# Pairwise bilinear interaction on one core: a ring of five x tiles, paired loads of x, four stores a tile, products in place

## The chip, the cores and the metric

The kernel runs on one core of a Trainium2 chip. The metric is the device time of one execution in microseconds (us). A core has a matrix engine (PE, or TensorE), which multiplies and transposes into PSUM, and VectorE (DVE), ScalarE (ACT) and GpSimd (POOL), which work element by element; GpSimd works on SBUF alone here. SyncE (SP) only issues transfers. 16 DMA engines move data between HBM and SBUF. Transfers issued by SP, by ScalarE and by GpSimd wait in three queues, and each DMA engine serves all three.

## The reference

```python
def _L0_rec_ref(inputs, W):                  # inputs (4096, 32, 64), W (496, 64, 64), float32
    F = inputs.shape[1]
    idx_i, idx_j = np.triu_indices(F, k=1)
    vi = inputs[:, idx_i, :]
    vj = inputs[:, idx_j, :]
    vidots = jnp.einsum('bpd,pde->bpe', vi, W)
    return vidots * vj
```

Every sample has 32 fields of 64 numbers. For each of the 496 pairs of fields (i, j), i < j, field i is multiplied by that pair's own 64 x 64 matrix, and the result, element by element, by field j. The output has 4096 x 496 x 64 numbers, 520 MB; the inputs have 42 MB.

## The kernel before

**Tiles.** 128 samples are a tile, one to a partition; there are 32 tiles, and two of them (NB = 2) are a block of 256 neighbouring samples, which is loaded by one transfer of 2 MB. `xpool` holds two blocks. The partition p of a block holds samples 2p and 2p + 1, so a partition's 16 KB lie together in HBM.

**Steps.** The work of a tile is a list of 46 steps (L169): step (g, i, c0, m) covers up to 16 pairs of one field i (CH = 16), the pairs p0[i] + c0 to p0[i] + c0 + m. A step has two matmuls (L259), one for each half of the 64 outputs, from the transposed x (`xT`) and the transposed weights (`wT`) into one PSUM tile `ps` of two banks (four such buffers, shared with the transposes). In the trace one such float32 matmul counts twice. Then the step multiplies by field j. For most steps DVE does this straight out of PSUM into the output tile `ot` (L279). For seven steps of a tile, those of `aside` with c0 = 0, ScalarE copies the PSUM tile to SBUF (L276) and GpSimd multiplies (L277). For the first three tiles the copy goes into `ot` itself and the product is made in place; for all others it goes into a spare tile `tmp` of `tpool`, which has four buffers.

**Output.** The 496 pairs are cut into five groups of 90 to 105 (`bounds`, L45). Each group of a tile has an `ot` of `opool`, which has three buffers, and one store by SP (L284). The very first group goes out in two stores.

**Transposed x.** `turn_x` (L153) transposes eight fields at a time on PE (L159), and ScalarE copies the result three times into an `xT` (L163 to L165) of four buffers. This is traced six steps (AHEAD) before the first step that needs it.

**Weights.** `load_w` loads W in four chunks of 128 rows, of which `cuts` says which are used: 0 to 128, 128 to 256, 256 to 368, 368 to 496. `order_w` (L139) reorders a quarter of a chunk on DVE, GpSimd or ScalarE, `turn_w` transposes it (L148) and copies it into `wT` (L151). `wT` has two tiles, rows 0 to 384 and the last 128, so that a step across row 368 takes two pairs of matmuls. The raw chunks lie in buffers of `opool`, in `wT` and in the last tile. A table of places in the schedule (L198) says when the quarters of chunks 1 to 3 are reordered and turned.

**The order of the work.** The schedule (L185) interleaves the first three tiles (LEAD) group by group, and then takes the tiles one by one. The framework orders each engine's instructions by this program and by what is ready, and puts in the waits for buffers; `keep_in_program_order` pins an instruction behind all that its engine was given before.

**Loads of x.** Blocks 0 and 1 are loaded by SP at the start, with W. Each later block is one load, traced at step 6 (LATE) of the first tile of the block before it (block 2 at step 6 of tile 3). Blocks 2, 3, 4, 6, 8, 10 and 12 are loaded by ScalarE's queue (L81), not pinned: in the trace they are issued when the last product that reads the buffer ends. Blocks 5, 7, 9, 11, 13, 14 and 15 (`fifteen`, L71) are loaded by GpSimd's queue, pinned, in four transfers (`load_fifteen`, L100): 120 partitions, a transfer of a few bytes (`turn_engines`, L97), and the last 8 partitions in two parts of 16 fields. The 120 partitions are spread over 15 DMA engines, so one engine is spared. In those blocks a gap of 64 bytes parts a partition's two samples.

Of the kernel before, what the change touches and what calls it, by code (L numbers as in the profile page):

```python
# [8 lines left out]
F32 = mybir.dt.float32  # L9
# [3 lines left out]
def kernel(  # L13
# [15 lines left out]

    nc = tc.nc  # L30

    B, F, D = x.shape
    P = 128
    NB = 2
    assert 2 * D == P and B % (NB * P) == 0
    NBLK = B // (NB * P)
    NP = F * (F - 1) // 2
    E2 = D // 2
    BANK = 512
    CH = BANK // E2  # L40
    RUN = 8
    p0 = [i * (F - 1) - i * (i - 1) // 2 for i in range(F)]


    bounds = [0, p0[3], p0[6] + CH, p0[11], p0[17], NP]  # L45
    groups = list(zip(bounds[:-1], bounds[1:]))
    cap = max(b - a for a, b in groups)

    aside = (1, 3, 5, 7, 9, 11, 13)

    cuts = [0, P, 2 * P, NP - P, NP]
    wrows = list(zip(cuts[:-1], cuts[1:]))

    const = ctx.enter_context(tc.tile_pool(name="const", bufs=1))
    xpool = ctx.enter_context(tc.tile_pool(name="xpool", bufs=2))
    xtpool = ctx.enter_context(tc.tile_pool(name="xtpool", bufs=4))
    tpool = ctx.enter_context(tc.tile_pool(name="tpool", bufs=4))
    opool = ctx.enter_context(tc.tile_pool(name="opool", bufs=3))
    psum = ctx.enter_context(tc.tile_pool(name="psum", bufs=4, space=bass.MemoryType.PSUM))

    ident = const.tile([P, P], F32, tag="ident", name="ident")
    make_identity(nc, ident)

    xs = {}
# [4 lines left out]


    fifteen = (5, 7, 9, 11, 13, 14, 15)  # L71

    def new_x(blk: int):
        gap = 16 if blk in fifteen else 0
        wide = xpool.tile([P, NB * (F * D + 16)], F32, tag="xs", name=f"xs_{blk}")
        wide = wide[:, : NB * (F * D + gap)].rearrange("p (k n) -> p k n", k=NB)
        xs[blk] = wide[:, :, : F * D].rearrange("p k (f d) -> p k f d", d=D)

    def load_x(blk: int, eng, k0: int = 0, k1: int = NB):
        src = rows_of(x, blk).rearrange("(p k) f d -> p k f d", k=NB)  # L80
        eng.dma_start(out=xs[blk][:, k0:k1], in_=src[:, k0:k1])  # L81
# [4 lines left out]
    SWR = 120  # L86
# [13 lines left out]
    def load_fifteen(blk: int):  # L100
        rows = rows_of(x, blk).rearrange("(p k) f d -> p k f d", k=NB)
        dst = xs[blk]

        def part(ps: slice, fs: slice):
            tc.keep_in_program_order(nc.gpsimd.dma_start(out=dst[ps, :, fs, :], in_=rows[ps, :, fs, :]))  # L105

        part(slice(0, SWR), slice(0, F))
        turn_engines(1)
        for h in range(2):
            part(slice(SWR, P), slice(h * F // 2, (h + 1) * F // 2))  # L110


    wflat = w.rearrange("p d e -> p (d e)")
    raw, wT = {}, {}
    EU = 2 * BANK // P
    NU = E2 // EU


    def home_of(c: int, r: int):
        home, tag, n = (wrows[3][0], "w3", P) if c == 3 else (0, "w", 3 * P)  # L120
        if home not in wT:
            wT[home] = const.tile([P, n, E2], F32, tag=tag, name=f"wT_{home}")
        return wT[home][:, wrows[c][0] - home : wrows[c][0] - home + r, :]

    def load_w(c: int):

        a = wrows[c][0]
        if c == 2:
            raw[c] = home_of(c, P).rearrange("p r e -> p (r e)")
        else:  # L130
            pool, tag = (const, "w3") if c == 3 else (opool, "ot")
            raw[c] = pool.tile([P, D * D], F32, tag=tag, name=f"raw_{c}")
        nc.sync.dma_start(out=raw[c], in_=wflat[a : a + P])

    def order_w(c: int, k: int, copy):
        r = wrows[c][1] - wrows[c][0]
        rp = tpool.tile([P, EU, 2, D], F32, tag="tmp", name=f"rp_{c}_{k}")
        src = raw[c][:r, :].rearrange("p (d h e) -> p e h d", h=2, d=D)
        ins = copy(rp[:r], src[:, k * EU : (k + 1) * EU])  # L139
        if c > 0:  # L140
            tc.keep_in_program_order(ins)
        return rp

    def turn_w(c: int, k: int, rp, copy):
        r = wrows[c][1] - wrows[c][0]
        pt = psum.tile([P, EU, P], F32, tag="ps", name=f"ptw_{c}_{k}")
        for n in range(EU):
            nc.tensor.transpose(  # L148
                pt[:, n, :r], rp[:r, n].rearrange("p h d -> p (h d)"), ident[:r, :r]
            )  # L150
        copy(home_of(c, r)[:, :, k * EU : (k + 1) * EU], pt[:, :, :r].rearrange("p e r -> p r e"))  # L151

    def turn_x(blk: int, k: int, q: int, copy):  # L153


        pt = psum.tile([P, RUN // 2, P], F32, tag="ps", name=f"ptx_{blk}_{k}_{q}")
        for u in range(RUN // 2):
            f = q * RUN + 2 * u
            nc.tensor.transpose(  # L159
                pt[:, u, :], xs[blk][:, k, f : f + 2, :].rearrange("p f d -> p (f d)"), ident  # L160
            )
        xT = xtpool.tile([P, 2, RUN // 2, P], F32, tag="xT", name=f"xT_{blk}_{k}_{q}")
        copy(xT[:, 0], pt)  # L163
        copy(xT[D:, 1], pt[:D])  # L164
        copy(xT[:D, 1], pt[D:])  # L165
        return xT


    steps = [  # L169
        (g, i, c0, min(CH, F - 1 - i - c0))  # L170
        for i in range(F - 1)
        for c0 in range(0, F - 1 - i, CH)
        for g, (a, b) in enumerate(groups)
        if a <= p0[i] + c0 < b
    ]
    NS = len(steps)
    first = {}
    for s, (_, i, _, _) in enumerate(steps):
        first.setdefault(i, s)

    LEAD = 3
    NT = NBLK * NB
    sched = [  # L185
        (t, s) for g in range(len(groups)) for t in range(LEAD) for s in range(NS) if steps[s][0] == g
    ]
    sched += [(t, s) for t in range(LEAD, NT) for s in range(NS)]
    place = {ts: n for n, ts in enumerate(sched)}


    AHEAD = 6
    due: dict = {}
    for t in range(NT):
        for q in range(F // RUN):
            at = place[t, first[q * RUN]] - AHEAD
            due.setdefault(max(0, at), []).append(("x", t // NB, t % NB, q))
    for c, orders, turns in (  # L198
        (1, (2, 4, 8, 10), (4, 7, 12, 15)),
        (2, (16, 18, 25, 27), (30, 33, 36, 39)),  # L200
        (3, (46, 48, 50, 52), (56, 59, 62, 65)),
    ):
        for k in range(NU):
            due.setdefault(orders[k], []).append(("order", c, k))
            due.setdefault(turns[k], []).append(("turn", c, k))
    LATE = 6
    loads = {place[blk * NB, LATE]: blk + 1 for blk in range(2, NBLK - 1)}
    loads[place[LEAD, LATE]] = 2

    new_x(0)  # L210
# [4 lines left out]
    new_x(1)  # L215
# [5 lines left out]
    v, p, a = nc.vector.tensor_copy, nc.gpsimd.tensor_copy, nc.scalar.copy  # L221
    xT, rps = {}, {}
    xT[0, 0, 0] = turn_x(0, 0, 0, a)
    due[0] = [d for d in due[0] if d != ("x", 0, 0, 0)]
# [5 lines left out]
    ots = {}  # L230
    for s, (t, st) in enumerate(sched):
        blk, kt = divmod(t, NB)
        g, i, c0, m = steps[st]
        if s in loads:
            new_x(loads[s])
            if loads[s] in fifteen:
                load_fifteen(loads[s])
            else:
                load_x(loads[s], nc.scalar)
        for what, *args in due.get(s, ()):  # L240
# [4 lines left out]
            else:  # L245
                c, k = args
                rps[c, k] = order_w(c, k, ((v, v, p, v), (v, v, p, a))[k % 2][c])

        base, end = groups[g]
        pa = p0[i] + c0  # L250
        if pa == base:
            ots[t] = opool.tile([P, cap, D], F32, tag="ot", name=f"ot_{t}_{g}")
        ot = ots[t]
        ps = psum.tile([P, 2, CH, E2], F32, tag="ps", name=f"ps_{s}")
        for lo, hi in ((0, wrows[3][0]), wrows[3]):
            home, lo, hi = lo, max(pa, lo), min(pa + m, hi)
            if lo < hi:
                for h in range(2):
                    nc.tensor.matmul(  # L259
                        ps[:, h, lo - pa : hi - pa, :],  # L260
                        xT[blk, kt, i // RUN][h * D : (h + 1) * D, (i + h) % 2, i % RUN // 2, :],
                        wT[home][h * D : (h + 1) * D, lo - home : hi - home, :],
                        start=True,
                        stop=True,
                    )
# [4 lines left out]
        xj = xs[blk][:, kt, j : j + m, :].rearrange("p m (h e) -> p m h e", h=2)  # L270
        if i in aside and c0 == 0:

            tmp = dst
            if t >= LEAD:
                tmp = tpool.tile([P, CH, 2, E2], F32, tag="tmp", name=f"tmp_{s}")
            nc.scalar.copy(tmp, src)  # L276
            nc.gpsimd.tensor_mul(dst, tmp, xj)  # L277
        else:
            nc.vector.tensor_mul(dst, src, xj)  # L279

        ends = (p0[2], end) if s < NS and (t, g) == (0, 0) else (end,)
# [34 lines left out]
```

## Time and profile before

| what | us |
|---|---|
| median of four runs | 1334.38 (1333.83 to 1335.27) |
| the profiled execution | 1334.23 |
| its span, first to last instruction | 1332.4 |
| loading before the first store moves | 0 to about 42 |
| three lead tiles, last store issued | 138.4 |
| last DVE product ends | 1316.2 |
| a store, issue to landing (min / median / max) | 9.6 / 16.6 / 22.8 |
| a ScalarE load of x, issue to landing (median) | 19.0 |
| a GpSimd load of x, 120 partitions (median) | 24.8 |
| DVE product of 16 pairs / 8 pairs / 1 pair (mean) | 1.22 / 0.68 / 0.21 |
| GpSimd product of 16 pairs (mean) | 2.36 |
| ScalarE copy of 16 pairs, into `tmp` / into `ot` (mean) | 1.012 / 1.013 |

563.13 MB move in 1332.4 us, 423 GB/s on average. A product's, a copy's or a store's time is that of one instruction or transfer; a transfer's runs from its issue until all its 16 engines have landed their part, with the time that it stands behind others in its queue.

### The profile page before, as it was taken

How to read it: one execution, taken by the hardware profiler on the slowest of the kernel's cores; microseconds unless marked ns; L12 is line 12 of the kernel's file. 1: busy time of each engine (PE TensorE's matmuls, PEld its weight loads, DVE VectorE, ACT ScalarE, POOL GpSimd, SP SyncE). 2: the span in 40 equal slices, each digit the busy share in tenths (PEclk: the TensorE clock that was granted, in tenths of full speed). 3: DMA queues.
4: the chain of work that ended last, by engine and by line, in shares of the span. 5: the costliest groups of instructions: out<-in, count | busy, mean ns of one | idle time of the engine just before them, and what ended most of it. 6: DMA issues, size and time to landing. Idle time of an engine off the chain costs nothing.

```text
span 1332.4 us, 16690 instructions
## 1 busy us (share of the span) xinstructions
PE 1132.5 (85%) x6656; PEld 601.2 (45%) x6656; DVE 950.5 (71%) x1258; ACT 471.6 (35%) x627; POOL 558.2 (42%) x264
## 2 busy tenths in 40 slices
PE   6989879978888888888888888888997988978894
PEld 4555444534444444444444444444443444444442
DVE  4878767757777677776767777676775777767784
ACT  4463323333333333333333333333333333333331
POOL 1752424444433444333453334542435443444441
PEclk9999989989999899999999999999999999989997
DMA  9999999999999999999999999999999999999998
GB/s 389 431 416 420 431 425 432 425 431 426 419 428 425 431 432 409 432 424 430 431 412 428 426 429 426 415 428 424 429 431 414 433 418 429 426 411 429 427 429 355
DMA packets 28142, 563.13 MB, mean 423 GB/s; under 512 B 3760, under 2 KB 3760, under 8 KB 4112
## 3 DMA queue, kind: packets, MB, share of 16 engines
q1 hardware_dynamic: 24192, 532.69, 94.1%
q0 software_dynamic: 2864, 14.70, 2.8%
q10 hardware_dynamic: 1008, 14.68, 2.6%
q8 instruction: 52, 0.85, 0.2%
q14 instruction: 26, 0.21, 0.0%
HBM read 41.94 MB, written 520.09 MB: 422 GB/s over the span
## 4 chain that ended last, share of the span: by engine, by line
DMA 56%; PE 18%; DVE 15%; POOL 4%; issue 4%; ACT 0%; DVEq 0%; POOLq 0%; SPq 0%; ACTq 0%
DMA out_dram<-ot 56%; PE ps L259 16%; DVE ot L279 15%; POOL ot L277 4%; PE ptx L159 1%; POOL rp L139 1%; ACT tmp L276 0%; DMA xs<-in_r_inputs_dram 0%; PE ptw L148 0%; DVE rp L139 0%; DVEq L279 0%; POOLq L277 0%; SPq L284 0%; DVEq L312 0%; ACTq L276 0%
## 5 line engine op out<-in xcount | busy, mean ns | idle before, releaser
L279 DVE TENSOR_TENSOR ot<-ps,xs 128x1024 f32<-128x1024 f32 (+15 forms) x1248 | 935.6, 806 | 351.5 <-DMA out_dram<-ot 213.2
L259 PE MATMUL ps<-wT,xT 64*128 64x512 f32 (+12 forms) x6016 | 1041.1, 485 | 168.1 <-DVE ot L279 162.8
L259 PEld LDWEIGHTS ps<-wT,xT 64*128 64x128 f32 x6016 | 531.0, 194 | 619.3 <-DVE ot L279 381.5
L277 POOL TENSOR_TENSOR ot<-tmp,xs 128x1024 f32<-128x1024 f32 x203 | 479.1, 2360 | 696.2 <-ACT tmp L276 516.2
L276 ACT COPY tmp<-ps 128x1024 f32<-128x1024 f32 x203 | 205.5, 1012 | 470.7 <-PE ps L259 434.4
L163 ACT COPY xT<-ptx 128x512 f32<-128x512 f32 x128 | 75.0, 586 | 323.5 <-PE ptx L159 323.5
L159 PE MATMUL ptx<-ident,xs 128*128 128x128 f32 x512 | 84.4, 288 | 9.3 <-DMA xs<-in_r_inputs_dram 5.8
L159 PEld LDWEIGHTS ptx<-ident,xs 128*128 128x128 f32 x512 | 53.9, 141 | 81.2 <-DVE ot L279 58.0
L165 ACT COPY xT<-ptx 64x512 f32<-64x512 f32 x128 | 74.5, 582 | 1.6
L164 ACT COPY xT<-ptx 64x512 f32<-64x512 f32 x128 | 73.9, 577 | 1.5
L277 POOL TENSOR_TENSOR ot<-ot,xs 128x1024 f32<-128x1024 f32 x21 | 49.9, 2379 | 51.4 <-ACT ot L276 51.3
L276 ACT COPY ot<-ps 128x1024 f32<-128x1024 f32 x21 | 21.3, 1013 | 24.3 <-PE ps L259 15.6
L148 PE MATMUL ptw<-ident,rp 128*128 128x128 f32 (+1 forms) x128 | 19.2, 306 | 5.8 <-DVE rp L139 5.8
L148 PEld LDWEIGHTS ptw<-ident,rp 128*128 128x128 f32 (+1 forms) x128 | 16.3, 160 | 13.9 <-DVE rp L139 5.2
L139 DVE COPY rp<-raw 128x1024 f32<-128x1024 f32 x9 | 14.7, 1655 | 10.6 <-DMA raw<-in_L_rec_W_dram 10.6
L151 ACT COPY wT<-ptw 128x1024 f32<-128x1024 f32 (+1 forms) x15 | 14.8, 984 | 13.1 <-PE ptw L148 11.7
L105 POOL DMA_DIRECT2D xs<-in_r_inputs_dram x21 | 13.3, 635 | 0.0
L97 POOL DMA_DIRECT2D scratch<-in_r_inputs_dram x9 | 8.2, 910 | 0.3 <-issue 0.3
L139 POOL COPY rp<-wT 112x1024 f32<-112x1024 f32 x4 | 7.9, 1976 | 0.0
L139 ACT COPY rp<-raw 128x1024 f32<-128x1024 f32 x3 | 6.0, 1991 | 1.9 <-DMA raw<-in_L_rec_W_dram 1.9
L151 DVE COPY wT<-ptw 128x1024 f32<-128x1024 f32 x1 | 1.2, 1225 | 3.5 <-PE ptw L148 3.5
L163 ACT ACT_TABLE_LOAD x1 | 1.3, 1283 | 0.7 <-PEq L303 0.7
(6 smaller groups left out, 0.9 us busy)
## 6 DMA issues: line engine op xcount, KB each, us to landing
out_dram<-ot SPq DMA_DIRECT2D x64, 3360.0 KB, 16.5
out_dram<-ot SPq DMA_DIRECT2D x32, 3168.0 KB, 15.7
out_dram<-ot SPq DMA_DIRECT2D x32, 3104.0 KB, 17.0
out_dram<-ot SPq DMA_DIRECT2D x31, 2880.0 KB, 17.0
xs<-in_r_inputs_dram ACTq DMA_DIRECT2D x7, 2048.0 KB, 19.0
xs<-in_r_inputs_dram POOLq DMA_DIRECT2D x7, 1920.0 KB, 24.8
raw<-in_L_rec_W_dram SPq DMA_DIRECT2D x3, 2048.0 KB, 13.8
xs<-in_r_inputs_dram SPq DMA_DIRECT2D x2, 1024.0 KB, 10.4
```

Of the source, the lines that this page charges most:

```text
L105: tc.keep_in_program_order(nc.gpsimd.dma_start(out=dst[ps, :, fs, :], in_=rows[ps, :, fs, :]))
L139: ins = copy(rp[:r], src[:, k * EU : (k + 1) * EU])
L148: nc.tensor.transpose(pt[:, n, :r], rp[:r, n].rearrange("p h d -> p (h d)"), ident[:r, :r])
L151: copy(home_of(c, r)[:, :, k * EU : (k + 1) * EU], pt[:, :, :r].rearrange("p e r -> p r e"))
L159: nc.tensor.transpose(pt[:, u, :], xs[blk][:, k, f : f + 2, :].rearrange("p f d -> p (f d)"), ident)
L163: copy(xT[:, 0], pt)
L164: copy(xT[D:, 1], pt[:D])
L165: copy(xT[:D, 1], pt[D:])
L259: nc.tensor.matmul(ps[:, h, lo - pa : hi - pa, :], xT[blk, kt, i // RUN][h * D : (h + 1) * D, (i + h) % 2, i % RUN // 2, :], wT[home][h * ...
L276: nc.scalar.copy(tmp, src)
L277: nc.gpsimd.tensor_mul(dst, tmp, xj)
L279: nc.vector.tensor_mul(dst, src, xj)
```

## The change

1. *x* lies in one tile `xb` of five places, one sample tile each (`starts`). Blocks 2e and 2e + 1 are loaded in the same tile of work, 4e - 1, the last tile of the two blocks before, which keeps the fifth place. `slot_of` says which two places a block takes, and the two tiles of a block in places 0 and 1 are taken in reverse order (`tile_of`).
2. GpSimd's load, now of every odd block from 3 on, is traced at step 4 of that tile; ScalarE's, of every even block from 2 on, three steps later, and pinned. The last 8 partitions of GpSimd's load come one sample at a time instead of 16 fields at a time.
3. The tiles after the lead have four groups of 118, 125, 127 and 126 pairs, and so four stores; field 15's 16 pairs are split at pair 370, so that these tiles have 47 steps. The three lead tiles have six groups of 72 to 91.
4. The output buffers are three places of one tile `ob`, of 127 pairs each (91 in the lead), against three of 105.
5. ScalarE's copy goes into the output tile everywhere, and GpSimd multiplies in place; `tpool` is gone.
6. `xT` has four buffers in the lead, two of them in the first place of `xb`, and two after it.
7. `wT` is one tile. The chunks of W are 0 to 112, 112 to 240, 240 to 368 and 368 to 496; each raw chunk lies where the next one's transposed form will go, the last one in `ob`, and the reordered quarters in `ob` too. Some quarters of chunks 2 and 3 have other places in the schedule.

The diff, cut to its core:

```diff
-    bounds = [0, p0[3], p0[6] + CH, p0[11], p0[17], NP]
-    groups = list(zip(bounds[:-1], bounds[1:]))
-    cuts = [0, P, 2 * P, NP - P, NP]
+    cuts = [0, NP - 3 * P, NP - 2 * P, NP - P, NP]
+    LEAD = 3
+    lead = [0, p0[3], p0[6], p0[9], p0[13], p0[18], NP]
+    later = [0, p0[4], p0[9], p0[15] + 10, NP]
...
-    xpool = ctx.enter_context(tc.tile_pool(name="xpool", bufs=2))
-    xtpool = ctx.enter_context(tc.tile_pool(name="xtpool", bufs=4))
-    tpool = ctx.enter_context(tc.tile_pool(name="tpool", bufs=4))
-    opool = ctx.enter_context(tc.tile_pool(name="opool", bufs=3))
...
+    wT = const.tile([P, NP, E2], F32, tag="wT", name="wT")
+    FD = F * D
+    GAP = 16
+    xb = const.tile([P, 5 * FD + 3 * GAP], F32, tag="xb", name="xb")
+    XT = 2 * (RUN // 2) * P
+    xtb = const.tile([P, 2 * XT], F32, tag="xtb", name="xtb")
+    ob = const.tile([P, 3 * cap1, D], F32, tag="ob", name="ob")
+    def out_home(n: int, later_: bool):
+        o, c = ((2 - n % 3) * cap1, cap1) if later_ else ((2 - n % 3) * cap0, cap0)
+        return ob[:, o : o + c, :]
+    def xt_home(t: int):
+        n = xt_used[0]
+        xt_used[0] += 1
+        n = n % 4 if t < LEAD else n % 2
+        mem, o = (xtb, n * XT) if n < 2 else (xb, (n - 2) * XT)
+        return mem[:, o : o + XT].rearrange("p (s u b) -> p s u b", s=2, b=P)
+    starts = [0, FD + GAP, 2 * FD + GAP, 3 * FD + GAP, 4 * FD + 2 * GAP]
+    def slot_of(blk: int):
+        e, second = divmod(blk, 2)
+        return ((1, 3), (2, 0))[e % 2][second]
+    def tile_of(t: int):
+        blk, k = divmod(t, NB)
+        return blk, 1 - k if slot_of(blk) == 0 else k
+    def x_block(blk: int):
+        o = starts[slot_of(blk)]
+        step = starts[slot_of(blk) + 1] - o
+        wide = xb[:, o : o + NB * step].rearrange("p (k n) -> p k n", k=NB)
+        return wide[:, :, :FD].rearrange("p k (f d) -> p k f d", d=D)
...
     def load_fifteen(blk: int):
-        part(slice(0, SWR), slice(0, F))
+        part(slice(0, SWR), slice(0, NB))
         turn_engines(1)
-        for h in range(2):
-            part(slice(SWR, P), slice(h * F // 2, (h + 1) * F // 2))
+        for k in range(NB):
+            part(slice(SWR, P), slice(k, k + 1))
...
-        (2, (16, 18, 25, 27), (30, 33, 36, 39)),
-        (3, (46, 48, 50, 52), (56, 59, 62, 65)),
+        (2, (16, 18, 26, 29), (24, 27, 32, 36)),
+        (3, (56, 58, 66, 72), (62, 68, 74, 78)),
...
-    LATE = 6
-    loads = {place[blk * NB, LATE]: blk + 1 for blk in range(2, NBLK - 1)}
-    loads[place[LEAD, LATE]] = 2
+    LATE = 4
+    loads = {place[2 * NB * e - 1, LATE]: 2 * e for e in range(1, NBLK // 2)}
...
         if s in loads:
-            new_x(loads[s])
-            if loads[s] in fifteen:
-                load_fifteen(loads[s])
-            else:
-                load_x(loads[s], nc.scalar)
+            load_fifteen(loads[s] + 1)
+        if s - 3 in loads:
+            tc.keep_in_program_order(load_x(loads[s - 3], nc.scalar))
...
         if i in aside and c0 == 0:
-            tmp = dst
-            if t >= LEAD:
-                tmp = tpool.tile([P, CH, 2, E2], F32, tag="tmp", name=f"tmp_{s}")
-            nc.scalar.copy(tmp, src)
-            nc.gpsimd.tensor_mul(dst, tmp, xj)
+            nc.scalar.copy(dst, src)
+            nc.gpsimd.tensor_mul(dst, dst, xj)
         else:
             nc.vector.tensor_mul(dst, src, xj)
```

## The prediction

> **What bounds the kernel now.** First the page's head, its slices and its list of DMA queues:
>
> ```profile
> span 1332.4 us, 16690 instructions
> ...
> PE 1132.5 (85%) x6656; PEld 601.2 (45%) x6656; DVE 950.5 (71%) x1258; ACT 471.6 (35%) x627; POOL 558.2 (42%) x264
> ...
> DMA  9999999999999999999999999999999999999998
> ...
> q1 hardware_dynamic: 24192, 532.69, 94.1%
> q0 software_dynamic: 2864, 14.70, 2.8%
> q10 hardware_dynamic: 1008, 14.68, 2.6%
> ```
>
> The DMA engines are busy in every slice, and the three queues add up to 99.5% of 16 engines' time. PE's 85% is mostly waiting work: it runs until its four PSUM tiles are full. Next the waits, to see who holds whom:
>
> ```profile
> DVE ot L279 <- DMA out_dram<-ot: 213.2, 97, 5.3
> ...
> POOL ot L277 <- DMA out_dram<-ot: 166.0, 66, 6.0
> ```
>
> The products wait for stores to land and free an output buffer, so the transfers set the pace. Time can be won only where the 16 engines spend theirs badly. Last the stretches: one without a load of x, one from ScalarE's issue of a load, one from GpSimd's, the one hole after the start, and the end:
>
> ```profile
> 210.00:260.00 50.00, 44.74 (x274) 23.88 (x274) 39.43 (x55) 17.56 (x25) 17.41 (x8) 0.97 1.00 431
> ```
> ```profile
> 423.50:453.50 30.00, 23.56 (x122) 11.79 (x120) 17.30 (x20) 9.67 (x13) 13.78 (x6) 0.89 1.01 427
> ```
> ```profile
> 511.70:541.70 30.00, 23.25 (x132) 11.94 (x131) 18.12 (x23) 11.06 (x15) 17.07 (x11) 0.94 1.00 414
> ```
> ```profile
> 90.00:92.00 2.00, 2.00 (x15) 0.96 (x12) 0.98 (x3) 1.37 (x2) 0.79 (x2) 1.00 0.63 266
> ...
> 1320.00:1332.40 12.40, 0.00 (x0) 0.00 (x0) 0.00 (x0) 0.00 (x0) 0.00 (x0) 0.50 0.53 228
> ```
>
> The last two columns are DMA share and GB/s. Nine stretches without a load (425 us) average 430 GB/s. The seven 30 us stretches from ScalarE's issues give 422, 424, 423, 427, 422, 425 and 419, mean 423; the seven from GpSimd's 416, 414, 414, 416, 415, 413 and 408, mean 414. The share stays at 1.00 throughout: the engines don't idle, their packets take longer. The end has share 0.53 over 12.4 us, 5.8 us idle on average: the last store's 16 engines finish between 1325.7 and 1331.1 us in the packet records, and the latest ends the kernel.
>
> **The change, part by part.** The sum is made against the profiled execution: 1334.23 us, span 1332.4 and 1.8 around it. The median of the four runs is 0.15 above that, which I leave out.
>
> *Four stores a tile.* Stores before: 32 x 5 and one more, 161. After: three lead tiles x 6, one more for the first, and 29 x 4, 135; so 26 fewer of equal bytes in all. In the packet records a 26,880 B packet takes a median of 996 ns and an 8,192 B one 309, so 0.0368 ns a byte and 8 ns a packet; the 4 B packet that ends each store on each engine takes 9. A store has 128 packets, 8 an engine: 8 x 8 + 9 = 73 ns. 26 x 73 ns = **-1.9 us** on each engine, nothing beside it to hide it, since the share is 1.00. The queue table bounds it: solving q1's and q0's rows for a cost per packet and per byte gives some 20 ns a packet, waits included, so 26 x 9 x 20 = -4.7; the other end is 0.
>
> The Trainium skill ("DMA: Bandwidth & Descriptors", Anatomy of one DMA) puts a fixed 2.0 us on each DMA. By that the 26 stores would be worth 52 us. Here the stretch 210 to 260 us has share 1.00 with stores queued behind one another, so the row decides and that cost is hidden.
>
> *Both loads together.* Bytes and number of loads stay: seven from ScalarE, seven from GpSimd. Measured against 430 GB/s, one of ScalarE's costs 7/430 x 30 = 0.47 us beyond its bytes, one of GpSimd's 16/430 x 30 = 1.1 us. The packet records show where: at 425.2 us, 1.7 us after ScalarE's issue, one store packet on nearly every engine is lengthened by 0.2 to 0.8 us, and within 3.5 us packets are back at 996 ns while the load runs on. It is a price of beginning to read, not of reading. After the change ScalarE's load is issued at step 7 of the tile and GpSimd's at step 4, whose first product (2.36 us) is in front of it; I put the two issues 1 to 3 us apart, so ScalarE's reads begin in the disturbance that GpSimd's already make. All of the smaller price saved is 7 x 0.47 = -3.3. No run of both at once is in the trace: none saved is 0, and if ScalarE's packets beside GpSimd's cost what GpSimd's do, 7 x (1.1 - 0.47) = +4.6. I take three quarters, **-2.5**, as the lengthened packets end so soon.
>
> The skill speaks against this term: the same page (Rules for kernel authors) says that DMAs from SP, ACT and GpSimd run on the same 16 engines and interleave, so that spreading them brings no bandwidth. By that rule the pairing is worth nothing and the sum is 1331.9. The rows above show a price per beginning, which the rule does not speak of.
>
> *Does the load still arrive?* Before, ScalarE's load had two tiles, some 80 us; GpSimd's too. After, block 2e is needed by the transposes at step 41 of the same tile: 34 of 47 steps of a tile that lasts 41 us of stores and 10 of loads, so 37 us. Alone it landed in 19.0 us. With three queues taking turns, 8 rounds of 32.5 + 16.4 + 8.2 KB an engine at 27 GB/s are 17 us instead of 13, so 23 to 25 to landing. Cover 12 us, then two queued stores, 19 us more. Block 2e+1 has two tiles longer. Cost 0. GpSimd's four issues (2.9 us around 349 us) delay the product of step 6 as they did before; ScalarE's takes 0.34.
>
> *Products in place, bigger buffers.* ScalarE's copy (1.01 us either way) now waits for the buffer's store to land; behind it in ScalarE's queue stand the copies of transposed x, and GpSimd's product (2.36) waits for it. So from landing to the next issue the four groups need: first, six DVE products, 6.2 us, beside ScalarE and GpSimd 6; second 6.5; third, three GpSimd products in a row of which the first starts 1 us after landing and the others wait for PE, 8.8; fourth, 16 DVE products, the traced 8.0 for the last 14 plus 1.05 and 0.5, 9.5. Sum 31 against 38 of transfer. The DMA has two stores of 9.4 us queued less the 6 us by which the slowest engine trails: 12.8. The slack is 3.3 or more, where today it is some 1 to 3 (two of 7.8 less 6, against 8). Cost 0. If the cover went, each us of fill beyond 12.8 would cost one per store. The ring's fifth tile and two xT buffers instead of four are covered alike: PE's last use of a buffer is two or more steps before its next transposes. The split at row 370 adds one DVE product a tile (0.82 + 0.55 for 1.22), hidden by DVE's 71%.
>
> *The lead.* GpSimd is busy without a gap from 40 to 61 us, by products and W's reordering copies. The four copies of chunk 2 come into a group of 81 pairs instead of 97: by the traced 2.36 and 1.97 us its stores go out at 50.9, 57.5 and 64.2, wanted at 52.9, 59.1 and 65.3: 1.1 us to spare. After it the groups have one GpSimd product (72 pairs), and chunk 3's work is due later, so the hole at 90 us, (1 - 0.63) x 2 = 0.74 us, should close. It rests the 13 faster engines rather than the last one, so **-0.4**; ends -0.75 and +2, if the 1.1 us aren't there.
>
> *The end* stays: the slowest engine still trails by 4 to 6 us, as instruction fetches and the seven loads that spare one engine are as many as before. Bounds -2 and +2.
>
> Sum: 1334.2 - 1.9 - 2.5 - 0.4 = **1329.4 us**.
>
> **The rivals.**
> (a) *Pairing saves nothing*, for ScalarE's reads still disturb the stores once. For it: GpSimd's stretches are still slow 10 to 20 us after the issue (418 and 421 GB/s between 520 and 540 us). Against: none of that comes after ScalarE's. 1334.2 - 1.9 - 0.4 = 1331.9, no change that can be told.
> (b) *Buffers become the bound*, slower: the third group's three copies wait for landing instead of going ahead into spare tiles, and their products end the store. For it: GpSimd's 166 us of waits for stores, and no spare left. Against: the slack of 4 us there. It decides where the third fill exceeds 12.8 us; at 13.1 it is 29 x 0.3 = 8.7 us, and 1340.6.
> (c) *The x load comes late.* It decides past 37 + 19 us from issue, where 25 are expected; 2 us beyond that, seven times, would give 1346.
> (d) *It gains more*: all 3.3, the whole hole, and 2 at the end: 1334.2 - 1.9 - 3.3 - 0.75 - 2 = 1326.3.
>
> **How the numbers follow.** Four runs spread over 1.4 us; under 0.2% (2.7 us) counts as no change, so faster means below 1331.7. The forecast has 0.58, (a) 0.20, (d) 0.10, (b) 0.08, (c) 0.04. Faster is forecast and (d), 0.68; same is (a); slower (b) and (c), 0.12. The range runs from just under (d), 1325.5, to (a) with the lead's bad end and the end's small loss, 1334.8; its outside holds (b), (c) and some of the rest.
>
> **What would show it.** 135 stores, most of 3.9 to 4.2 MB; GpSimd's and ScalarE's issues 1 to 3 us apart; the 30 us from them at about 413 GB/s (1.1 + 0.1 us lost of 30), not at 407 (1.6 us lost); no hole at 90 us; stores' waits on DVE and POOL that still leave a share of 1.00. The prediction is wrong if the share falls below 0.97 in the middle (b), if PE waits for x (c), or if the paired stretches lose 1.6 us or more each (a).

## The result, and the profile after

| | before | after |
|---|---|---|
| median of the runs, us | 1334.04 (1332.29 to 1337.19, 53 runs) | 1335.52 (1333.22 to 1337.79, 33 runs) |
| ratio, 95% interval | | 1.0011 [1.0006, 1.0015] |
| the profiled execution, us | 1334.23 | 1334.21 |
| its span, us | 1332.4 | 1332.4 |

The change is worth +1.5 us, slower by less than the 0.2% that counts as no change; 1329.4 was forecast, and the measured time lies just above the range. The profiled execution after is 1.3 us under its own median, that of before 0.2 over its. So the two profiles account for a difference of nothing, against a forecast of -4.8 us, and not for the last 1.5.

The page of after, the lines that answer to those of before (DMA is the busy share of each of 40 slices in tenths):

```profile
span 1332.4 us, 17377 instructions
...
PE 1145.6 (86%) x6644; PEld 598.5 (45%) x6644; DVE 952.0 (71%) x1287; ACT 471.6 (35%) x627; POOL 558.4 (42%) x264
...
DMA  9999999999999999999999999999999999999997
...
q1 hardware_dynamic: 20576, 532.69, 93.5%
q10 hardware_dynamic: 1008, 14.68, 2.9%
q0 software_dynamic: 2640, 14.70, 2.8%
```

Transfers still set the pace. The stores' queue q1 has 3616 packets fewer for the same bytes and takes 0.6% less of 16 engines' time; ScalarE's queue q10 takes 0.3% more for the same packets and bytes. The span is the same.

The waits, of engines and of SP:

```profile
DVE ob L314 <- DMA out_dram<-ob: 179.1, 78, 7.2
...
ACT ob L311 <- DMA out_dram<-ob: 121.2, 46, 8.9
```
```profile
SPq L319 <- DVE ob L314: 1133.2, 135, 19.4
SPq L319 <- POOL ob L312: 122.9, 94, 3.9
```

The wait for a store to land that GpSimd had (166 us) is now ScalarE's, as the copy goes into the output buffer; SP's 135 waits are the 135 stores.

The stretches: first the start, then 30 us from the issue of each of the seven pairs of loads (the last two columns are DMA share and GB/s, the one ahead of them is PE's clock):

```profile
90.00:140.00 50.00, 49.00 (x328) 27.51 (x328) 40.97 (x66) 21.02 (x30) 13.83 (x6) 1.00 0.99 421
...
139.00:141.00 2.00, 2.00 (x12) 0.91 (x12) 1.30 (x3) 0.00 (x0) 0.00 (x0) 1.00 0.67 269
150.00:155.00 5.00, 5.00 (x32) 3.11 (x34) 4.61 (x6) 2.22 (x3) 4.80 (x3) 1.00 1.02 298
```
```profile
145.00:175.00 30.00, 23.72 (x134) 12.59 (x132) 19.38 (x26) 11.15 (x15) 17.00 (x11) 0.91 1.00 384
299.60:329.60 30.00, 21.71 (x104) 11.20 (x100) 13.48 (x18) 9.28 (x12) 14.76 (x10) 0.77 1.00 423
463.40:493.40 30.00, 20.93 (x106) 10.84 (x104) 13.71 (x18) 9.37 (x12) 14.80 (x11) 0.83 1.00 417
627.30:657.30 30.00, 21.14 (x108) 11.13 (x104) 13.84 (x18) 9.38 (x12) 15.02 (x11) 0.83 1.01 412
791.10:821.10 30.00, 21.18 (x108) 11.18 (x104) 13.85 (x18) 9.39 (x12) 15.07 (x11) 0.83 1.00 404
953.50:983.50 30.00, 20.77 (x110) 10.51 (x108) 14.37 (x20) 9.37 (x12) 15.42 (x11) 0.83 1.00 410
1116.90:1146.90 30.00, 20.02 (x110) 10.07 (x108) 14.62 (x20) 9.42 (x12) 15.64 (x11) 0.89 1.01 404
```

Against 430 GB/s the first pair loses (430 - 384) / 430 x 30 = 3.2 us, the other six, of mean 412, 1.28 each; together 10.9 us. In the kernel before, seven loads of each kind by themselves lost 7 x (0.47 + 1.1) = 11.0. The first pair is alone with that price: at 150 to 155 us the share is full, but it is the loads' reads with hardly a store packet beside them, at 298 GB/s. No store is queued then, because the lead's last groups fill more slowly than they are stored: the same shortage leaves the hole at 139 to 141 us. In the issues and packet records the stores of those groups, and the first one behind them, are issued 1.5 and 0.3 us ahead of the end of the store before, and then 0.3 and 2.8 us after it.

The end, the same 4.6 us in both kernels, before and then after:

```profile
1326.20:1330.80 4.60, 0.00 (x0) 0.00 (x0) 0.00 (x0) 0.00 (x0) 0.00 (x0) 0.50 0.19 82
```
```profile
1326.20:1330.80 4.60, 0.00 (x0) 0.00 (x0) 0.00 (x0) 0.00 (x0) 0.00 (x0) 0.50 0.05 21
```

One engine of 16 is a share of 0.06. Before, three engines still store at the end; after, one does (0.05), and the others are done. The packet records give it engine by engine: summed packet durations over 16 (called the work of the mean engine here), and the times at which the 16 engines end their part of the last store:

| profiled run | mean work | 8th engine ends | 15th | last |
|---|---|---|---|---|
| before | 1328.3 | 1326.2 | 1330.9 | 1331.1 |
| after | 1326.1 | 1322.9 | 1326.0 | 1330.9 |

The mean engine has 2.2 us less to do, and most engines end 3 us sooner; the last end is where it was. In a quiet stretch of after (825 to 950 us) nine in ten of the packets of 32,256 B take the same 1194 ns within 10, and about a sixteenth of them take some 25 to 60 ns longer. A packet starts 3 to 4 ns before the one ahead of it on its engine ends, so packets can be strung together to engines: the long ones are nearly all on one engine, called the slow engine from here on. With 40 ns more on each of a store's eight packets it falls 0.33 us behind per store. The lag of the last engine of a store behind the 8th grows to between 8 and 9 us ahead of each of the last three pairs of loads, and falls across each of the seven pairs, by 0.5 to 2.6 us at the first four and by 3.5 to 5.7 at the last three. This fits GpSimd's load, whose 120 partitions go to fifteen engines and spare one.

### The profile page after: what moved, and what is told of

Read it like the earlier page. It is cut to its first block, busy times and chain, and to the rows that moved or that the text cites. A ratio compares the mean times of both kernels' runs of the same rounds, so it can differ in the third digit from the quotient of the medians.

```text
span 1332.4 us, 17377 instructions
## 1 busy us (share of the span) xinstructions
PE 1145.6 (86%) x6644; PEld 598.5 (45%) x6644; DVE 952.0 (71%) x1287; ACT 471.6 (35%) x627; POOL 558.4 (42%) x264
## 4 chain that ended last, share of the span: by engine, by line
DMA 47%; PE 23%; DVE 10%; issue 10%; POOL 5%; ACT 3%; DVEq 0%; ACTq 0%; POOLq 0%; SPq 0%
DMA out_dram<-ob 47%; PE ps L298 21%; DVE ob L314 10%; POOL ob L312 4%; ACT ob L311 2%; PE ptx L200 2%; POOL xb L152 0%; PE ptw L191 0%; DMA xb<-in_r_inputs_dram 0%; POOL ob L181 0%; DVE ob L181 0%; POOL scratch L144 0%; DVEq L314 0%; ACT xtb L202 0%; ACT xtb L204 0%
## 5 line engine op out<-in xcount | busy, mean ns | idle before, releaser
L314 DVE TENSOR_TENSOR ob<-ps,xb 128x1024 f32<-128x1024 f32 (+4 forms) x1277 | 939.9, 791 | 346.6 <-DMA out_dram<-ob 179.1
L298 PE MATMUL ps<-wT,xtb 64*128 64x512 f32 (+15 forms) x5760 | 1014.6, 490 | 146.1 <-DVE ob L314 74.8
L312 POOL TENSOR_TENSOR ob<-ob,xb 128x1024 f32<-128x1024 f32 x224 | 529.2, 2368 | 743.9 <-ACT ob L311 713.5
L298 PEld LDWEIGHTS ps<-wT,xtb 64*128 64x128 f32 x5760 | 507.9, 194 | 618.1 <-DVE ob L314 259.1
L311 ACT COPY ob<-ps 128x1024 f32<-128x1024 f32 x224 | 226.8, 1013 | 486.6 <-PE ps L298 321.7
L202 ACT COPY xtb<-ptx 128x512 f32<-128x512 f32 x122 | 71.5, 586 | 309.6 <-PE ptx L200 307.9
L200 PE MATMUL ptx<-ident,xb 128*128 128x128 f32 x512 | 86.1, 292 | 10.5 <-DMA xb<-in_r_inputs_dram 5.8
L200 PEld LDWEIGHTS ptx<-ident,xb 128*128 128x128 f32 x512 | 55.1, 144 | 61.7 <-issue 37.4
L204 ACT COPY xtb<-ptx 64x512 f32<-64x512 f32 x122 | 71.0, 582 | 3.0
L203 ACT COPY xtb<-ptx 64x512 f32<-64x512 f32 x122 | 70.4, 577 | 2.9
L298 PE MATMUL ps<-wT,xb 64*128 64x512 f32 (+15 forms) x244 | 42.3, 465 | 3.3 <-DVE ob L314 1.5
L192 ACT COPY wT<-ptw 128x1024 f32<-128x1024 f32 (+1 forms) x15 | 14.9, 993 | 10.5 <-PE ptw L191 10.4
## 6 DMA issues: line engine op xcount, KB each, us to landing
xb<-in_r_inputs_dram ACTq DMA_DIRECT2D x7, 2048.0 KB, 22.6
```

The source lines that it names most:

```text
L192: copy(wT[:, a:b, k * EU : (k + 1) * EU], pt[:, :, :r].rearrange("p e r -> p r e"))
L200: nc.tensor.transpose(pt[:, u, :], x_tile(t)[:, f : f + 2, :].rearrange("p f d -> p (f d)"), ident)
L298: nc.tensor.matmul(ps[:, h, :m, :], xT[t, i // RUN][h * D : (h + 1) * D, (i + h) % 2, i % RUN // 2, :], wT[h * D : (h + 1) * D, pa : pa + ...
L311: nc.scalar.copy(dst, src)
L312: nc.gpsimd.tensor_mul(dst, dst, xj)
```

## The experiments

All are compared with the kernel before; "+" and "-" are against the kernel after unless said otherwise. Where nothing is said, the computation is the same.

**GpSimd's load later: first_late, apart, no_relief.** Every load of GpSimd one tile later than ScalarE's (apart); only that of block 3 (first_late, `- (e > 1)` in the key); as apart, but with `load_x(odd[s], nc.scalar)` for the last line, so that ScalarE issues them on all 16 engines (no_relief).

```diff
+    odd = {place[2 * NB * e, LATE]: 2 * e + 1 for e in range(1, NBLK // 2)}
-        if s in loads:
-            load_fifteen(loads[s] + 1)
+        if s in odd:
+            load_fifteen(odd[s])
```

> The changed kernel with GpSimd's first load (block 3) one tile later, at step 4 of tile 4; the other six pairs stay. In the changed kernel the first pair's 30 us moved 384 GB/s, 3.2 us lost, while no store was queued, and the engine that this load spares had nothing to do. Theory L (one DMA engine trails, only its work sets the end): it gains what it idled there, 2 to 3 us: 1332.5 to 1333.5, ratio 0.998 to 0.999, and it trails by 5 to 6 us at the end instead of 8. Theory M (all engines' mean work sets the end): about 1.5 us, 1334, and the trailing stays 8 us. If the first pair is harmless: 1335.5, ratio 1.001.

Measured 1336.89 us (11 runs), ratio 1.0016 [1.0007, 1.0025]: +1.4, where both theories had a gain. The last engine ends at 1333.2, while fifteen end by 1326.8. The place stays dear for ScalarE's load alone, (430 - 406) / 430 x 30 = 1.7 us where such a load cost 0.47 before:

```profile
145.00:175.00 30.00, 27.71 (x178) 14.72 (x176) 24.11 (x35) 12.88 (x18) 14.22 (x7) 1.00 1.01 406
```

> The changed kernel with every GpSimd load one tile later than ScalarE's, so that no two loads run together. If pairing saves what the prediction said (2.5 us of 3.3), it is 2.5 us slower than the run with the first load alone moved: about 1335.5. If pairing saves next to nothing, as the paired stretches of the changed kernel say (1.56 us lost a pair, against 0.47 + 1.1 before), it equals that run within 0.5 us. If pairs cost more where no store is queued (1.7 us and more in the pairs of 791, 953 and 1117 us), it is 1 to 2 us faster than that run.

Measured 1334.23 us (11 runs), ratio 0.9999 [0.9990, 1.0008]: -1.3, and 2.7 below first_late, more than any of the three cases had. Two of its stretches, from ScalarE's issue and from 7 us ahead of GpSimd's:

```profile
299.60:329.60 30.00, 22.81 (x110) 12.01 (x106) 14.18 (x18) 9.56 (x12) 12.58 (x7) 0.77 1.01 431
339.00:369.00 30.00, 26.52 (x154) 13.87 (x154) 20.89 (x29) 10.91 (x14) 18.06 (x11) 0.94 1.00 403
```

ScalarE's costs nothing here and GpSimd's (430 - 403) / 430 x 30 = 1.9 us, against 0.5 for the pair at the same place in after. Over all fourteen stretches ScalarE's loads lose 2.7 us and GpSimd's 12.1, together 14.9 against the 10.9 of the seven pairs: in this profiled run loads apart are dearer for the mean engine (mean work 1328.8, +2.7) and the time is not. The engines end closer together, 1325.2 to 1328.6 and one at 1330.7.

> The changed kernel with the odd blocks too loaded by ScalarE's queue, one tile after the even ones, 128 partitions over all 16 DMA engines; no load spares an engine. Theory L (one engine, whose packets of a store take some 40 ns longer than the others' 1194, sets the end): that engine gets 7 x 131 KB more, at 0.038 ns a byte 35 us, the others 2.3 us less: 1365 to 1370, while the other 15 engines wait for it. Theory M (mean work of 16 engines): the same work, 1333 to 1335.

Measured 1354.67 us (4 runs), ratio 1.0150 [1.0136, 1.0164]: 20.4 us over apart, for the same bytes; far more than theory M had, and 10 to 15 us short of theory L. The end of its span:

```profile
1344.90:1351.20 6.30, 0.00 (x0) 0.00 (x0) 0.00 (x0) 0.00 (x0) 0.00 (x0) 0.50 0.06 26
```

One engine of 16 stores for 6.3 us alone. The mean work is 1330.6, 1.8 us above apart, and the time 20.4: no mean of the engines makes this kernel's time, the one that trails does. All sixteen must land their part before a buffer comes free, so the others also wait for it on the way: from 440 us on the lag stays between 6 and 9 us outside the loads instead of growing with each, as fifteen engines wait.

**Is the lag made by instruction fetches? fetch.** Ten dummy matmuls of one pair more in a tile, so that PE's program is longer (57 packets of instructions against 52).

```diff
-        for h in range(2):
+        for h in range(-1 if st % 5 == 0 else 0, 2):
+            if h < 0:
+                nc.tensor.matmul(
+                    ps[:, 0, :1, :],
...
+                continue
```

> The changed kernel with 10 more narrow matmuls a tile (one pair wide, overwritten by the real one), 320 in all, 82 KB of PE instructions more, so 5 more instruction fetches of 16 KB at 0.94 us. Theory L with the fetches all on the trailing engine: 4 to 5 us later, 1339.5 to 1340.5, trailing by 12 to 13 us. If the fetches are spread over the 16 engines: 0.3 us later. PE's own 0.1 to 0.3 us a matmul, 1 to 3 us a tile, has slack in every tile.

Measured 1336.61 us (11 runs), ratio 1.0019 [1.0010, 1.0028]: +1.1, not the 4 to 5 us of theory L and more than the 0.3 of the other case, within the spread of these kernels. The last store ends on fifteen engines by 1329.6 and on the last at 1334.6, a gap of 5.0 as in after (4.9). The steps of the lag don't fall on the fetches. The fetches are not shown to make it.

**More loads that spare an engine: relief_14, apart_relief_14, before_relief_12, apart_spare_14, apart_spare_3, apart_spare_7.** A block of ScalarE's goes to GpSimd: block 14 in halves of one sample (relief_14, paired with 15; apart_relief_14, not paired), or with a gap behind each of the five places, in GpSimd's usual form (apart_spare_14; blocks 6, 10 and 14 in apart_spare_3; all seven even blocks in apart_spare_7); in the kernel before, block 12.

```diff
+        if s in loads and loads[s] in (14,):
+            load_fifteen_halves(loads[s])
-        if s - 3 in loads:
+        if s - 3 in loads and loads[s - 3] not in (14,):
```
```diff
-    fifteen = (5, 7, 9, 11, 13, 14, 15)
+    fifteen = (5, 7, 9, 11, 12, 13, 14, 15)
```
```diff
-    starts = [0, FD + GAP, 2 * FD + GAP, 3 * FD + GAP, 4 * FD + 2 * GAP]
+    starts = [n * (FD + GAP) for n in range(5)]
...
+        if s in loads and loads[s] in (14,):
+            load_fifteen(loads[s])
```

> The changed kernel with block 14 too loaded by GpSimd's queue, 120 partitions over 15 DMA engines, so that the spared engine is spared once more (131 KB, 4.8 us); the other 15 get 0.3 us more each. Theory L: the end comes 3 to 4.8 us earlier, 1331 to 1332.5, and the last engine trails by some 3 us instead of 8. Theory M: the mean is unchanged, 1335.5.

Measured 1344.99 us (5 runs), ratio 1.0079 [1.0066, 1.0092]. It told another thing than was asked. GpSimd's queue in it (start, duration, instruction, idle before):

```profile
1121.56 0.98 POOL L144 DMA_DIRECT2D scratch<-in_r_inputs_dram  x1
1135.51 1.07 POOL L152 DMA_DIRECT2D xb<-in_r_inputs_dram  x2 [12.97 <-DMA xb<-in_r_inputs_dram]
1136.60 4.66 POOL L323 TENSOR_TENSOR ob<-ob,xb 128x1024 f32<-128x1024 f32 x2
```

With two loads of 2 MB in a row the issuing instruction waits 13 us, and behind it stand GpSimd's products, so the store of that group goes out late. In this form two GpSimd loads can't be paired.

> The kernel with the loads apart, and block 14 too loaded by GpSimd's queue over 15 engines; block 15 a tile later, so that GpSimd's queue is not filled by two loads in a row (which held its products, and so a store, until 1139 us in the run with block 14 and the loads paired). Theory L: the slow engine ends 4.8 us earlier, and the next ones, which ended 2.1 us before it with the loads apart, set the end: about 1332, 1.5 to 2.5 below the 1334.2 of loads apart. Theory M: 1334.2.

Measured 1339.13 us (5 runs), ratio 1.0038 [1.0026, 1.0051]: 4.9 over apart. The lag did not drop at this load: rows of one sample in this form did not spare the engine that trails. A miss of the experiment's form, not a test of the theory.

> The kernel before with block 12 loaded by GpSimd's queue over 15 engines instead of ScalarE's over 16. Theory L with one slow engine: it is spared 4.8 us more; in the kernel before the last three engines ended at 1331.1, 1330.9 and 1329.6, so the next one sets the end, 0.2 to 1.5 us earlier plus 0.3 for its greater share, and GpSimd's load costs 0.65 us more than ScalarE's: 1333.5 to 1335, no clear change. If all three trail for want of relief: 3 to 4 us faster.

Measured 1334.07 us (11 runs), ratio 1.0003 [0.9994, 1.0012]: no change, though in its profiled run (span 1330.0) the last engine ended at 1328.5, 2.6 us sooner than in before.

> The kernel with the loads apart, a gap between all five places of x (so that ScalarE's loads have packets of 8 KB, 16 an engine instead of 8, 0.5 us more in all), and block 14 loaded by GpSimd in the same form as the odd blocks, so that the slow engine is spared once more. (The earlier try cut that load by samples, 120 rows of one sample each, and the slow engine's lag did not fall behind it.) Theory L: 4.8 us less for the slow engine less some 2 us that a GpSimd load seems to cost it, and the next engine ended 2.1 us before it: 1332 to 1333. Theory M: 1334.7 to 1335.5.

Measured 1333.47 us (11 runs), ratio 0.9995 [0.9986, 1.0004]: 0.8 under apart, 2.1 under after, and not told from before.

> Edit: apart, the gaps between all five places of the ring, and blocks 6, 10 and 14 too by GpSimd on fifteen engines (ten loads that spare an engine instead of seven). Theory (one engine trails and ends the kernel; a load that spares it nets it 2.1 us): the last engine gains up to 3 x 2.1 = 6.3 us against apart, the other fifteen lose about 3 x 1 us, so the gap of some 4 us at the end closes and the time falls by 1 to 3 us against apart, to 1331 to 1333; the last engine's end of the last store comes within 2 us of the others'. Rival (all engines are alike, a load by GpSimd costs 1.1 us where ScalarE's costs 0.5): 3 x 0.6 = 2 us slower than apart, 1336.

Measured 1334.67 us (12 runs), ratio 1.0006 [0.9997, 1.0014]: neither the gain of the theory nor the loss of the rival. Its last engines end at 1330.3, 1331.0 and 1331.7, the other thirteen by 1327.8. The packets of those three have the usual length: with the slow engine spared more often, others are just as late.

> Edit: as before this, with all seven even blocks by GpSimd too (fourteen loads that spare an engine). Theory: the trailing engine is then no longer last; it gains 14 us less the wait for the others, and the other fifteen set the end with 7 x 1 to 1.5 us more work than in apart, from a mean end of some 1326.5 to 1334 to 1337 of span: 1335 to 1339 us, all sixteen engines ending within 3 us. Rival (engines alike): 7 x 0.6 = 4 us slower than apart, 1338, with the same spread of the engines' ends as in apart. The end of the last store engine by engine tells them apart, not the time alone.

Measured 1341.49 us (5 runs), ratio 1.0051 [1.0039, 1.0063]: worse than both. Three engines end last again (1337.5 to 1339.4), and two stretches from the issues of GpSimd's loads of an even and an odd block lose (430 - 415) / 430 x 30 = 1.0 and 2.7 us:

```profile
468.00:498.00 30.00, 23.66 (x131) 11.80 (x130) 18.11 (x24) 11.08 (x15) 17.01 (x11) 0.94 1.00 415
514.70:544.70 30.00, 25.31 (x146) 12.98 (x144) 20.25 (x27) 11.13 (x15) 17.03 (x11) 0.94 0.99 392
```

In these runs sparing one engine pays only until the next ones are as late, which seven to eight such loads about reach.

**How many stores: five_stores, six_stores, apart_five.** The tiles after the lead in five groups as before, or in the lead's six (`later = lead`); apart_five has the five and GpSimd's loads of apart.

```diff
-    later = [0, p0[4], p0[9], p0[15] + 10, NP]
+    later = [0, p0[3], p0[6] + CH, p0[11], p0[17], NP]
-    cap1 = max(b - a for a, b in groups[LEAD])
+    cap1 = 127
```

> The changed kernel with five groups and stores a tile after the lead too, cut as before (90, 97, 99, 105, 105 pairs), in the same places of 127: 29 stores more. The prediction's term: 29 x 73 ns = 2.1 us slower than the changed kernel, 1337.6, if nothing else depends on it. If smaller stores also take cover (two of 7.8 us queued instead of two of 9.5, less the 8 us by which the slow engine trails), the other 15 engines run dry more often, but the slow one does not: by theory L still 1337 to 1338, by theory M 1339 and more.

Measured 1333.71 us (11 runs), ratio 0.9995 [0.9986, 1.0004]: -1.8, where four stores were to be the faster.

> The changed kernel with the lead's six groups (90, 81, 72, 82, 80, 91 pairs) for all tiles: 58 stores more than the changed kernel, 29 more than with five. By the price per packet alone (73 ns a store on each engine) it is 4.2 us slower than the changed kernel, 1339.7, and 2.1 slower than whatever five stores take. If a smaller store is worth more than its packets, as the run with five said (1.8 us faster than four), it stays at 1333 to 1334.

Measured 1335.86 us (11 runs), ratio 1.0015 [1.0006, 1.0024]: +0.3. The packet price is there: 522 packets an engine more than after, mean work 1331.8, +5.7 us. The time is not, and it fits neither case: the engines end between 1327.9 and 1332.0, closer together than in any other of these runs but the last engine hardly later than after's. This run and no_relief are the two that tell mean work and time apart, one from each side.

> The changed kernel with GpSimd's loads one tile later than ScalarE's and with five groups and stores a tile after the lead: two parts undone at once. Alone the first gave 1334.23 and the second 1333.71, against 1335.52 of the changed kernel. If they cost by separate ways they add up: 1335.5 - 1.3 - 1.8 = 1332.4, ratio 0.999. If both only give the 15 faster engines back what they lose beside reads while no store is queued, they overlap: 1333.5 to 1334.2, ratio 1.000.

Measured 1336.99 us (11 runs), ratio 1.0021 [1.0011, 1.0030]: +1.5. Five stores and loads apart each came out faster alone, and slower together. I can't explain this from the traces.

**In place: before_in_place.** The kernel before with the copy into the output tile and the product in place everywhere.

```diff
-            if t >= LEAD:
+            if t >= NT:
```

> The kernel before with one part of the change: ScalarE's copy goes into the output tile everywhere and GpSimd multiplies in place; the four spare tiles serve W alone. If waiting for the buffer lengthens the fills, the stores go out later where only 0.5 to 3 us were to spare, the 15 faster engines run dry more often, and by theory L the slow one does not: 1334 to 1335. If the copy's wait holds up the slow engine as well: 1337 and more. If the prediction's cover holds: 1334.0.

Measured 1334.33 us (11 runs), ratio 1.0003 [0.9994, 1.0012]: nothing, as predicted for after.

## Why the prediction was wrong, point by point

**What bounds the kernel: right, but read too coarsely.** The transfers do. But "the 16 engines" were costed as one. A store ends with the engine that is last, and in after's quiet stretch the long packets belong to one engine all along.

**Four stores a tile, -1.9: right as packets, too large as time of an engine, and nothing at the end.** 135 stores came, and 240 packets an engine fewer (1760 to 1520). The summed work of the mean engine fell by 2.2 us; 240 packets at 8 ns are 1.9 of it. But packets overlap by 3 to 4 ns, so the sum counts some time twice: from the earliest of the 16 ends of one tile's last store to that of the next, the shortest tiles take 37.56 us before, 37.52 after, 37.56 in five_stores and 37.61 in six_stores, 0.04 to 0.05 a store and not 0.073. And by the latest of the 16 ends a tile without a load takes 38.8 to 39.0 us with five stores as with four: for the engine that sets the pace there, no gain from the fewer stores can be seen. The section of the Trainium skill that the prediction names here ("DMA: Bandwidth & Descriptors", Anatomy of one DMA) gives its 2.0 us for DMAs that GpSimd issues; these stores are SP's.

**Both loads together, -2.5: as work -0.1 to -2.7, by what it is set against, and in time no gain.** ("I take three quarters, as the lengthened packets end so soon.") The issues were 0.1 us apart and not 1 to 3, as GpSimd came to its load only when ScalarE did:

```profile
299.62 0.33 ACTq L128 DMA_DIRECT2D xb<-in_r_inputs_dram  x1
```
```profile
299.70 0.83 POOL L152 DMA_DIRECT2D xb<-in_r_inputs_dram  x1
```

Against the kernel before it saved next to nothing: the packets' time beyond 8 ns and 0.0368 ns a byte, summed over the run and divided by 16, fell by 0.35 us, and the stretches give 10.9 against 11.0. Six pairs cost 1.28 us, near the 1.2 forecast and under the 1.57 of two loads apart; that is -1.7. The first costs 3.2, 1.6 more than two apart, and takes it back. Against apart, which undoes this part alone, pairing saved the mean engine 2.7 us (4.0 by the stretches), about what was forecast; and apart is 1.3 us the faster. So the price of work was not far off, and it did not become time. The test named for rival (a), a loss of 1.6 us or more in each paired stretch, is met by three of the seven; their mean is 1.56.

**The lead, -0.4: the sign is wrong.** The hole at 90 us closed, as forecast. The step stopped there and did not follow the lead to its end, where three tiles in turn store their last 91 pairs: they are issued 8.1 us apart, 13 steps each, for a transfer of 2.98 MB / 430 GB/s = 6.9. The hole at 139 us, (1 - 0.67) x 2 = 0.66 us, and the first pair's 3.2 - 1.28 = 1.9 over the others are its price; less the 0.74 of the closed hole that is +1.8. first_late has one load at that place and still pays 1.7 for it, so the place is dear for one load too; that the empty queue makes it so is argued, as no kernel was run with another lead.

**Load in time, in place, bigger buffers, 0: right.** ScalarE's loads landed in 22.6 us where 23 to 25 were forecast, no transpose waits for x after the start, and before_in_place prices the copies at nothing. (b) and (c) did not come.

**The end stays: this is the step that failed.** It said that "the slowest engine still trails by 4 to 6 us, as instruction fetches and the seven loads that spare one engine are as many as before". The fetches are not shown to be its source, and the loads that spare an engine were as many, yet the last engine ends 8.0 us behind the 8th after, against 4.9 before: of the 3.3 us that the 8th gained, the last kept 0.2. no_relief shows that such an engine can set the time: seven loads without the sparing and 20.4 us.

The latest ends of the stores show how. Four tiles with one load of each kind take 162.6 to 163.7 us before and 161.9 to 163.9 after, where four tiles without a load take 155.6: there, pairing gave next to nothing. Near 1175 us both kernels are level. Before has one GpSimd load left to pay there (a tile of 43.1 us, which puts it 3.7 us behind), but its last three tiles then take 37.6 us each, 112.7 together; those of after take 38.4 to 38.95, 116.2 together. Followed back packet by packet, the engine that ends last in after takes 33 to 70 ns too long on its packets from 1302 to 1312 us, and the last ones of first_late, fetch and no_relief take some 30 to 80 ns too long likewise: it is the slow engine. The last three of before and the last one of apart have packets of the usual length but for single ones, over the same time before their ends. So "the slowest engine" was not the same engine in the two kernels: the prediction took its lag over from a kernel that, in its profiled execution, does not end on the slow engine.

Why it does so after and not before is argued, not shown. The last of GpSimd's loads is issued at 1117 us after, at 1164 before and at 1162 in apart, and the slow engine falls 0.33 us further behind with each store that follows. No run moves that one load alone, and before_in_place, with the loads of before, ends on a slow engine at 1331.0 and takes the same time.

**What stays open.** The 1.5 us by which after's median is slower than before's: the profiled execution doesn't hold them. Ten of the variants lie between 1333.5 and 1337.0 in an order that neither packets, nor pairs, nor mean work explain (apart_five above all); the lag is a saw-tooth, and where its teeth stand at the end differs with each. And which engine is slow, and why: the records don't name it. Its packets take the usual time again once the last product has ended (at 1312.0 us in after, where they are usual from 1314; at 1332.4 in no_relief, from 1334), so the delay goes with the work of the core's engines; no run tells which part of it, nor whether the recording of the profile has a share in it. The Trainium skill ("DMA: Bandwidth & Descriptors", Latency and other measured facts) says that engines 7 and 15 are usually slower in traces, and offers as a best guess that GpSimd's descriptor rings crowd a port. Here it is one of 16, by some 40 ns of 1194, and whether it is one of those two can't be read. A slow engine trails in no_relief too, where GpSimd's queue moved 64 packets in the whole run: there the guess does not hold.

No version beat both kernels by more than its interval. apart_spare_14 (1333.47) and five_stores (1333.71) are faster than after and the same as before.

## What to carry to other kernels

When the transfers bound a kernel, cost the engine that ends last, not the mean of the 16: look at the DMA share of the last 10 us, where 0.06 for some microseconds means one engine alone, and ask of each edit whether it takes work from that one, and whether the same engine will be last behind it. Here fewer packets and cheaper reads only let the others wait longer. And when a prologue is rearranged, follow its queue of stores to the last group, not to the first hole that closes.

## What was unexpected of the hardware

- One DMA engine is some 3.4% slower a packet than the others in the stretches read (some 40 ns on 1194), with 32,256 B packets as with 26,880 B ones (24 to 50 ns on 996), and is as fast as they are once the last product has ended.
- A store stream moves 430 GB/s; the two reading queues, with hardly a store packet beside them, 298 at 150 to 155 us.
- Two GpSimd loads of 2 MB in a row blocked GpSimd's instruction stream for 13 us in relief_14, products and all.
- Seven loads moved from fifteen engines to sixteen, with the same bytes, cost 20.4 us.
